# Summing the eight factors of a matrix on TensorE as stacks of 16 rows by 8 factors, with a new order of the first steps

## The chip, the cores and the metric

The kernel runs on one core of a Trainium2 chip. The metric is the time of one execution on the device in microseconds (us). Times of single stretches come from one profiled execution, whose profile is called the page, and from questions put to its trace. PE is TensorE, PEld its weight load, DVE VectorE, ACT ScalarE, POOL GpSimd, SP SyncE.

## The reference

All data are float32. Eight batches of 1024 rows of 1024 numbers (x), a memory of 64 rows for each batch with a mask, eight factor matrices of 1024 x 1024 and a bias.

```
scores = (layernorm(x) @ memory^T) / sqrt(1024), masked
x = x + softmax(scores) @ memory
x = x + (sum over r of layernorm(x) @ factors[r]) / sqrt(8) + bias
```

The eight factors are applied to the same rows, so their sum W can be made once (33.5 MB are read for a matrix of 4.2 MB) and each row is multiplied by W alone.

## The kernel before

The 8192 rows are worked on in 16 groups of 512 rows: four tiles of 128 rows, numbered t, or two halves q of 256 rows. Two groups make up a batch and share its memory. A group goes through these steps: its rows are loaded (load_rows, and from group 2 on a second time in another layout by load_blocks); their mean and variance are taken; the rows are transposed; scores and softmax against the memory; read_out multiplies the weights by the memory; residual adds that to x in place; norm_sums and norm_squares (ACT, half a group each, with the last steps on POOL) take the second layernorm's statistics; normalize (ACT) writes the normalized rows h. For PE, h must stand transposed. In group 0 PE does this (transpose_h_pe, copies by ACT). From group 1 on relayout (L575) moves h by 16 transfers of 64 KB on SP's queue into a tile hb, and transpose_rows (DVE) transposes blocks of 32x32 into hT.

The product with W is done by a scheme with seven half-size products in place of eight (numbers 1 to 7, with sums s1 to s4 of quarters of hT by combine_rows and sums t1 to t4 of quarters of W). W's quarters and their combinations stand in seven tiles, wq: b11, b21, b22, t1, t2, t3, t4, each of 128 x 4 x 512. Products 2 to 5 are split once more into seven parts of a quarter of the size (combine_parts, part, give_part; combine_factors makes their right sides, on DVE); in the first groups product 5 is done whole instead. product (L614) needs b11 for number 1, t1 for 5, t2 for 6 and t3 for 7; t2, t3, t4, b21 and b22 need all of the factors. give adds a product to x, add_bias (POOL) adds the bias, store writes the tile.

The order is written out by hand. START is a table of steps, run once; it holds groups 0 and 1, the factors and the beginning of group 2. LOOP is a table run for each group g, with steps of the group before (p), the next (n) and the next but one (m). Each engine and each queue takes its instructions in the order of these tables, and SP issues all transfers but the first memory, the mask and the bias, which ACT issues. Every transfer gets one of eight completion semaphores in turn.

Room is given out by Slots, first returned first taken. There are ten large buffers of 1 MB (bigs) for factors, h, hb, hT, and the transposed or block-wise x, and eight PSUM banks (banks). A step that takes a buffer waits for the step that returned it.

The factors before: load_factor s r (L700) reads a quarter s of the rows of factor r, 1 MB in one transfer with 8 KB for each partition. The eight terms of a quarter are added in two ways, as the table says: add_factor (L706) adds two loaded tiles, or one to the sum so far, on DVE; sum_factor (L724) multiplies by the identity on PE, four matmuls of 512 columns that accumulate in four PSUM banks, and add_sums (L739) adds these on DVE. START has 12 sum_factor and 20 add_factor steps, and one of the relayouts of group 1 comes after the last load_factor, the other later still.

```
load_factor 2 0; add_bias 0 0 3; add_factor 2 3; part 0 4 2; load_factor 2 5;
combine_parts 0 4 2; add_factor 2 1; sum_factor 2 0; product 0 1 5; combine_rows 0 0 4;
add_factor 2 4; give_part 0 4 2; combine_parts 0 4 3; load_memory 2; load_rows 2 0;
normalize 1 0 1; relayout 1 0; add_factor 2 5; centre_memory 2; normalize 1 1 0; add_sums 2 1;
product 0 0 6; load_blocks 2 1; add_sums 2 0; add_bias 0 1 3; give 0 0 6; transpose_memory 2;
```

Of the kernel before, what the change touches and what calls it, by code (L numbers as in the profile page):

```python
# [24 lines left out]
load_rows 1 0; constants; load_rows 0 0; load_rows 0 1; load_rows 0 2; load_memory 0;  # L25
row_stats 1 0; load_rows 1 1; transpose_x_pe 0 0; row_stats 0 0; centre_memory 0; load_rows 0 3;
transpose_x_pe 1 0; load_rows 1 2; masks; transpose_memory 0; load_factor 0 5; add_factor 0 5;
row_stats 0 1; load_factor 1 6; transpose_x_pe 0 1; load_rows 1 3; row_stats 1 1; scores 0;
scores_back 0; row_stats 0 2; load_factor 1 3; transpose_x_pe 1 1; row_stats 0 3;
load_factor 0 2; softmax 0; load_factor 1 1; scores 1; row_stats 1 2; row_stats 1 3;  # L30
add_factor 1 6; weights_back 0; scores_back 1; read_out 0 0 0; add_factor 0 2; read_out 0 1 0;
softmax 1; read_out 0 0 1; residual 0 0 0; residual 0 0 1; load_factor 1 2; load_factor 1 0;
load_factor 0 6; read_out 0 1 1; load_factor 1 5; weights_back 1; norm_sums 0 0; add_factor 1 3;
residual 0 1 1; load_factor 1 7; residual 0 1 0; add_factor 0 6; add_factor 1 7; sum_factor 1 0;
add_factor 1 2; load_factor 1 4; sum_factor 1 1; norm_squares 0 0; read_out 1 1 0;
load_factor 0 7; load_factor 0 3; read_out 1 0 1; load_factor 0 4; normalize 0 0 0;
normalize 0 0 1; norm_sums 0 1; sum_factor 1 4; residual 1 1 0; load_factor 3 7; add_factor 0 7;
transpose_h_pe 0 0 0; read_out 1 0 0; residual 1 0 0; norm_squares 0 1; load_factor 3 5;
read_out 1 1 1; residual 1 0 1; sum_factor 1 5; transpose_h_pe 0 0 1; load_factor 0 0;
residual 1 1 1; add_sums 1 1; load_factor 0 1; add_sums 1 0; add_factor 0 3; combine_rows 0 0 1;  # L40
sum_factor 3 5; add_factor 0 1; norm_sums 1 1; sum_factor 3 7; normalize 0 1 0; sum_factor 0 4;
normalize 0 1 1; add_factor 0 0; load_factor 3 3; load_factor 3 2; sum_factor 3 3; norm_sums 1 0;
combine_rows 0 0 2; add_sums 0 1; load_factor 3 4; norm_squares 1 0; load_factor 3 6;
add_factor 3 2; transpose_h_pe 0 1 0; add_sums 0 0; load_factor 3 0; load_factor 3 1;
add_factor 3 4; load_factor 2 3; load_factor 2 6; load_factor 2 1; add_factor 3 0;
add_factor 3 1; normalize 1 0 0; transpose_h_pe 0 1 1; load_bias; product 0 0 5; load_factor 2 2;
give 0 0 5; sum_factor 3 6; load_factor 2 7; add_bias 0 0 2; norm_squares 1 1; load_factor 2 4;
combine_rows 0 1 1; product 0 0 1; combine_rows 0 0 3; add_factor 2 6; product 0 1 1;
add_sums 3 1; combine_parts 0 4 1; add_sums 3 0; sum_factor 2 2; give 0 1 1; give 0 0 1;
sum_factor 2 7; load_factor 2 0; add_bias 0 0 3; add_factor 2 3; part 0 4 2; load_factor 2 5;  # L50
combine_parts 0 4 2; add_factor 2 1; sum_factor 2 0; product 0 1 5; combine_rows 0 0 4;
# [16 lines left out]
scores_back 2; give 0 1 7; combine_factors 5; give_part 0 2 6; part 0 3 6; part 0 2 2;  # L68
row_squares 2 1; softmax 2; give_part 0 3 6; combine_parts 0 3 4; part 0 3 5; give 0 1 5;
part 0 2 7; give_part 0 2 7; part 0 3 2; store 0 3; add_bias 0 0 1; give_part 0 3 5;  # L70
give_part 0 2 2; add_bias 0 1 0; add_bias 1 0 2; part 0 3 7;
"""

LOOP = """
# [749 lines left out]
```

## Time and profile before

| what | value |
|---|---|
| times of 3 runs | 941.76, 943.79, 947.74 us; median 943.79 |
| span of the profiled execution | 939.8 us |
| PE busy | 916.9 us, 98% of the span |
| DVE, ACT, POOL busy | 783.4, 458.9, 265.2 us |
| DMA in the first four fortieths of the span (94 us) | 313, 421, 420, 421 GB/s |
| factor transfers | 32 of 1024 KB, median 11.4 us from issue to landing |
| relayout transfers | 480 of 64 KB, median 2.0 us from issue to landing |

The median of the times is 4.0 us above the profiled span. Busy time of PE is modelled from the starts of pipelined matmuls. A float32 matmul shows as two records, one for each pass, so the 48 matmuls of the 12 sum_factor steps are 96 rows of the profile. The rows that matter are shown with the prediction.

### The profile page before, as it was taken

To read this page: it belongs to the slowest core of one execution; us is meant where nothing else is said; L and a number is where in the kernel's file an instruction comes from. 1 tells how busy PE (TensorE), PEld (TensorE's weight loads), DVE (VectorE), ACT (ScalarE), POOL (GpSimd) and SP (SyncE) were. 2 spreads that over 40 slices of the span, in tenths; PEclk is the share of its full clock that TensorE was granted. 3 is DMA by queue.
4 is the path that set the end of the run, shared out by engine and by line. 5 is a ranking of instruction groups with operands and counts; after the bars stand their busy time and mean duration, and the time that the engine had idled before them with its cause. 6 is when DMAs were issued, how large, how long until landed. Compare 5 with 4: busy or idle time off the path is not lost.

```text
span 939.8 us, 11731 instructions
## 1 busy us (share of the span) xinstructions
PE 916.9 (98%) x3637; PEld 578.2 (62%) x3637; DVE 783.4 (83%) x1619; ACT 458.9 (49%) x836; POOL 265.2 (28%) x355
## 2 busy tenths in 40 slices
PE   4899999999999999999999999999999999999998
PEld 4444456756657565666656575665756666665766
DVE  4799998969698896969698897969889797979876
ACT  4573233638464463737555373836545464745100
POOL 0202023515133231514233151513323151423221
PEclk9999999999999999999999999999999999999999
DMA  8999767476574847467484846558484856641412
GB/s 313 421 420 421 205 160 187 139 164 177 142 188 122 213 136 165 146 166 191 122 199 125 206 145 159 157 148 202 121 193 139 182 153 157 171 134 57 128 46 89
DMA packets 93565, 167.04 MB, mean 178 GB/s; under 512 B 12352, under 2 KB 71872, under 8 KB 89408
## 3 DMA queue, kind: packets, MB, share of 16 engines
q1 hardware_dynamic: 93024, 165.20, 61.9%
q10 hardware_dynamic: 480, 1.12, 0.4%
q8 instruction: 28, 0.46, 0.2%
q14 instruction: 33, 0.27, 0.1%
HBM read 101.25 MB, written 33.55 MB: 143 GB/s over the span
## 4 chain that ended last, share of the span: by engine, by line
PE 92%; DMA 6%; DVE 1%; ACT 1%; issue 0%; SPq 0%; POOL 0%; DVEq 0%
PE yu L621 34%; PE ro L496 6%; PE y5u L671 6%; PE y2u L671 6%; PE y4u L671 6%; PE y3u L671 6%; PE scT L428 6%; DMA f<-in_L_ffn_factors_dram 5%; PE y3v L671 3%; PE y5v L671 3%; PE y2v L671 3%; PE y4v L671 3%; PE sum L734 2%; PE y3z L671 1%; PE y2z L671 1%; PE y5z L671 1%
## 5 line engine op out<-in xcount | busy, mean ns | idle before, releaser
L570 POOL TENSOR_TENSOR x<-x,bias_bc 128x512 f32<-128x512 f32 x128 | 170.2, 1342 | 130.0 <-DVE x L685 51.6
L589 DVE STREAM_TRANSPOSE hT<-hb 128x1024 f32<-128x1024 f32 x60 | 72.7, 1231 | 59.7 <-DMA hb<-h 55.4
L532 ACT ACTIVATE junkz<-x 128x1024 bf16<-128x1024 f32 x64 | 67.6, 1057 | 109.0 <-DVE x L504 108.0
L621 PE MATMUL yu<-t,s 128*128 128x512 f32 x256 | 115.3, 593 | 1.9 <-DVE t L750 1.9
L621 PE MATMUL yu<-b,hT 128*128 128x512 f32 x256 | 114.9, 592 | 0.0
L621 PE MATMUL yu<-t,hT 128*128 128x512 f32 x256 | 112.6, 592 | 0.0
L563 ACT ACTIVATE h<-x,nb,rstd 128x512 f32<-128x512 f32 x128 | 96.5, 825 | 24.8 <-POOL rs L335 13.5
L504 DVE SCALAR_TENSOR_TENSOR x<-ro,rden,x 128x512 f32<-128x512 f32 x128 | 88.6, 746 | 13.2 <-PE ro L496 13.0
L634 DVE SCALAR_TENSOR_TENSOR x<-yu,x 128x512 f32<-128x512 f32 x128 | 82.8, 678 | 3.3 <-PE yu L621 3.2
L621 PEld LDWEIGHTS yu<-t,hT 128*128 128x128 f32 x256 | 48.6, 190 | 54.0 <-issue 52.6
L385 DVE STREAM_TRANSPOSE xT<-xb 128x256 f32<-128x256 f32 x224 | 81.6, 411 | 0.0
L621 PEld LDWEIGHTS yu<-t,s 128*128 128x128 f32 x256 | 48.5, 190 | 50.6 <-issue 46.3
L543 ACT ACTIVATE junky<-x,zm 128x1024 bf16<-128x1024 f32 x64 | 73.5, 1149 | 11.1 <-POOL zm L330 8.5
L621 PEld LDWEIGHTS yu<-b,hT 128*128 128x128 f32 x256 | 48.6, 190 | 48.4 <-issue 46.9
L330 POOL TENSOR_SCALAR zm<-zs 128x2 f32<-128x2 f32 x28 | 9.8, 351 | 223.9 <-ACT junkz L532 223.9
L347 ACT ACTIVATE junk<-x 128x1024 bf16<-128x1024 f32 x56 | 58.9, 1052 | 26.1 <-DMA x<-in_x_dram 25.2
L359 ACT ACTIVATE junk<-x,nmean 128x1024 bf16<-128x1024 f32 x56 | 64.3, 1148 | 7.1 <-POOL nmean L330 4.9
L496 PE MATMUL ro<-mem,eT 64*128 64x512 f32 x256 | 64.8, 615 | 0.6 <-DVE x L504 0.4
L428 PE MATMUL scT<-xT,memT 128*64 128x256 f32 x512 | 58.8, 382 | 0.0
L685 DVE SCALAR_TENSOR_TENSOR x<-y3u,x 128x256 f32<-128x256 f32 x64 | 26.7, 418 | 37.5 <-PE y3u L671 30.3
L428 PEld LDWEIGHTS scT<-xT,memT 128*64 128x64 f32 x512 | 35.3, 137 | 21.1 <-issue 4.3
L734 PE MATMUL sum<-f,ident 128*128 128x512 f32 x96 | 42.8, 597 | 2.3 <-DMA f<-in_L_ffn_factors_dram 2.1
(148 smaller groups left out, 1631.5 us busy)
## 6 DMA issues: line engine op xcount, KB each, us to landing
x<-in_x_dram SPq DMA_DIRECT2D x64, 512.0 KB, 3.5
f<-in_L_ffn_factors_dram SPq DMA_DIRECT2D x32, 1024.0 KB, 11.4
out_dram<-x SPq DMA_DIRECT2D x64, 512.0 KB, 3.1
hb<-h SPq DMA_DIRECT2D x480, 64.0 KB, 2.0
xb<-in_x_dram SPq DMA_DIRECT2D x112, 256.0 KB, 7.5
mem<-in_ctx_dram SPq DMA_DIRECT2D x14, 256.0 KB, 6.3
mem<-in_ctx_dram ACTq DMA_DIRECT2D x2, 256.0 KB, 9.4
bias_bc<-in_L_ffn_bias_dram ACTq DMA_DIRECT2D x1, 512.0 KB, 8.1
```

What stands on the lines that cost most here:

```text
L385: nc.vector.transpose(xT[:, 2 * e + c].rearrange("p (t j) -> p t j", j=Q), xb.rearrange("p t (k e i c) -> p e c t k i", e=NC // 2, i=2, c= ...
L428: nc.tensor.matmul(ps[ts(h, M), : 2 * P], mT[:, c, :], st["xT", g, h][:, c, :], start=(c == 0), stop=(c == NC - 1),)
L496: nc.tensor.matmul(ps, eT[ts(h, M), q, :], m[ts(h, M), ts(n, H)], start=True, stop=True)
L504: nc.vector.scalar_tensor_tensor(xt, st.pop(("ro", g, q, n, h)), rden[:, k : k + 1], xt, ALU.mult, ALU.add)
L532: nc.scalar.activation(junk, st["x", g, 2 * h + q], AF.Copy, accum_out=s1[:, h : h + 1])
L543: nc.scalar.activation(junk, st["x", g, 2 * h + q], AF.Square, bias=nmean[:, h : h + 1], accum_out=ss[:, h : h + 1])
L563: nc.scalar.activation(to, fr, AF.Identity, bias=nb[:, h : h + 1], scale=rstd[:, h : h + 1])
L570: eng.tensor_add(xt, xt, bias_bc[:, ts(k % 2, H)])
L589: nc.vector.transpose(st["hT", g, q][:, h].rearrange("p c (t j) -> p t c j", j=Q), hb[:, h].rearrange("p t (c i) -> p t c i", i=Q),)
L621: nc.tensor.matmul(ps, lhs[:, c, :], wq[right][:, c, :], start=(first and c == 0), stop=(c == KH - 1), skip_group_check=True,)
L634: nc.vector.scalar_tensor_tensor(xt, st["y", g, q, key], ISR, xt, ALU.mult, ALU.add)
L671: nc.tensor.matmul(ps, lhs[:, c, :], right[:, c, :], start=(first and c == 0), stop=(c == 1), skip_group_check=True,)
```

## The change

load_stack takes the place of load_factor. A stack is one transfer's worth of 16 rows of all eight factors: partition 8k + r holds row k (of the 16) of factor r, 4 KB. A load_stack fills one buffer of 1 MB with two stacks, by two transfers of 512 KB. add_stack takes two buffers (four stacks) and adds the eight factors within each stack by a matmul with a 0/1 matrix of 128 x 32 (stack0 for the even, stack1 for the odd of 32 output rows); the four stacks go to four strips of 32 partitions of the same PSUM bank, for both halves of the columns: 8 matmuls. Two add_stacks (i = 0, 1) complete two banks. take_sums moves these into wq: b11, b21 and b22 by copies on ACT, t1 and t2 by subtractions on DVE straight from PSUM. subtract_factors makes t3 and t4. add_factor, sum_factor and add_sums are gone.

START is written anew. Its first part, up to the first steps of the parts of group 0, is shown below. In it both relayouts of group 1 stand among the load_stacks: 19 of the 32 come ahead of relayout 1 0, four between the two, nine after relayout 1 1. Products 1 and 5 of group 1 are done whole and stand ahead of the last add_stack. The memory is loaded ahead of the mask. LOOP holds the same steps in another order (so product 6 of half 0, and part 3 4's combine_parts, have moved over the loop's end into the next round). s2 gets a buffer for each half, in the room of mask8f.

```diff
+load_rows 0 1; load_rows 0 2; load_rows 0 0; load_memory 0; constants; load_rows 0 3;
+row_stats 0 0; row_stats 0 1; load_rows 1 0; centre_memory 0; transpose_x_pe 0 0; load_rows 1 2;
+transpose_x_pe 0 1; masks; row_stats 1 0; transpose_memory 0; row_stats 0 2; load_stack 0 0 0 1;
+load_rows 1 1; load_rows 1 3; load_stack 0 1 0 1; row_stats 1 1; scores 0; load_stack 1 0 0 1;
+row_stats 0 3; transpose_x_pe 1 1; row_stats 1 2; scores_back 0; transpose_x_pe 1 0; softmax 0;
+scores 1; weights_back 0; scores_back 1; load_stack 0 0 0 0; read_out 0 0 0; row_stats 1 3;
+read_out 0 0 1; load_stack 0 1 0 0; load_stack 0 1 1 0; load_stack 0 1 1 1; softmax 1;
+load_stack 0 0 1 0; load_stack 1 1 0 0; load_stack 0 0 1 1; add_stack 0 0 0; read_out 0 1 0;
+residual 0 0 0; read_out 0 1 1; residual 0 0 1; add_stack 0 1 0; norm_sums 0 0; residual 0 1 1;
+residual 0 1 0; norm_squares 0 0; load_stack 2 0 0 0; norm_sums 0 1; weights_back 1;
+norm_squares 0 1; read_out 1 0 1; residual 1 0 1; read_out 1 0 0; add_stack 0 0 1;
+normalize 0 0 0; residual 1 0 0; load_stack 1 1 0 1; load_stack 1 0 0 0; normalize 0 0 1;
+normalize 0 1 0; add_stack 0 1 1; transpose_h_pe 0 0 0; transpose_h_pe 0 0 1; take_sums 0 0;
+read_out 1 1 1; norm_sums 1 0; combine_rows 0 0 1; norm_squares 1 0; residual 1 1 1;
+normalize 0 1 1; load_stack 1 0 1 0; transpose_h_pe 0 1 0; add_stack 1 0 0; load_stack 1 1 1 1;
+transpose_h_pe 0 1 1; load_stack 1 0 1 1; combine_rows 0 0 2; load_stack 1 1 1 0;
+add_stack 1 1 0; add_stack 1 0 1; read_out 1 1 0; normalize 1 0 0; normalize 1 0 1;
+take_sums 1 0; residual 1 1 0; load_stack 2 1 1 1; load_stack 2 1 0 1; relayout 1 0;
+add_stack 1 1 1; take_sums 1 1; norm_sums 1 1; load_stack 2 0 0 1; combine_rows 0 0 3;
+take_sums 0 1; combine_rows 0 1 1; combine_rows 0 1 3; norm_squares 1 1; load_stack 2 1 0 0;
+transpose_rows 1 0 0; normalize 1 1 0; product 0 1 1; product 0 0 1; product 0 0 5;
+transpose_rows 1 0 1; load_stack 2 0 1 1; add_stack 2 0 0; load_stack 3 0 0 1; product 0 1 5;
+add_stack 2 1 0; give 0 1 5; normalize 1 1 1; relayout 1 1; load_stack 2 1 1 0; product 1 0 1;
+transpose_rows 1 1 0; combine_parts 0 4 1; combine_rows 0 1 2; take_sums 2 0;
+transpose_rows 1 1 1; load_stack 2 0 1 0; product 1 1 1; combine_rows 1 0 1; add_stack 2 0 1;
+load_bias; load_stack 3 0 0 0; add_stack 2 1 1; combine_parts 0 4 2; combine_rows 1 1 1;
+load_stack 3 1 0 0; take_sums 2 1; give 0 0 5; combine_rows 0 0 4; load_stack 3 1 0 1;
+load_stack 3 0 1 1; load_stack 3 0 1 0; product 1 1 5; give 0 1 1; add_stack 3 0 0; give 0 0 1;
+give 1 1 1; add_stack 3 1 0; load_stack 3 1 1 0; add_bias 0 0 3; add_bias 1 1 1; product 1 0 5;
+combine_factors 5; take_sums 3 0; subtract_factors 0; load_stack 3 1 1 1; add_stack 3 0 1;
+give 1 0 5; add_stack 3 1 1; add_bias 0 1 3; give 1 1 5; take_sums 3 1; load_rows 2 1;
+combine_factors 3; product 0 1 6; product 0 0 6; subtract_factors 1; part 0 4 2; load_memory 2;
+add_bias 0 1 2; add_bias 0 1 1; combine_factors 4; give 0 0 6; part 0 4 1; combine_parts 0 4 3;
+give 0 1 6; part 0 4 5; give_part 0 4 1; product 0 0 7; centre_memory 2; load_blocks 2 1;
+combine_parts 0 4 4; combine_factors 2; give_part 0 4 2; part 0 4 6; give 1 0 1; give_part 0 4 6;
...
@@ -175,10 +175,16 @@
     neghalf = const.tile([P, 4], F32, name="neghalf")
     nc.gpsimd.memset(neghalf, -0.5)
 
+    stack = [const.tile([P, 2 * P // R], F32, name=f"stack{i}") for i in range(2)]
+    for i in range(2):
+        nc.vector.memset(stack[i], 0.0)
+        nc.vector.tensor_reduce(
+            stack[i].rearrange("p (k i) -> p i k", i=2)[:, i], ident.rearrange("p (k r) -> p k r", r=R), AX.X, ALU.add
+        )
+
 
 
     mask8 = const.tile([B, P // M, M], mask.dtype, name="mask8")
-    mask8f = const.tile([B, P], F32, name="mask8f")
     maskT = const.tile([P, B], F32, name="maskT")
     valid = const.tile([P, B], F32, name="valid")
     bias_bc = const.tile([P, D], F32, name="bias_bc")
...
@@ -601,7 +606,7 @@
             ops["s1"] = work.tile([P, KH, P], F32, tag=f"s1{q if 5 in SECOND else ''}", name=f"s1_{g}_{q}")
             nc.vector.tensor_add(ops["s1"], ops["a21"], ops["a22"])
         if k == 2:
-            ops["s2"] = work.tile([P, KH, P], F32, tag="s2", name=f"s2_{g}_{q}")
+            ops["s2"] = work.tile([P, KH, P], F32, tag=f"s2{q}", name=f"s2_{g}_{q}")
             nc.vector.tensor_sub(ops["s2"], ops["s1"], ops["a11"])
         if k == 3:
             nc.vector.tensor_sub(ops["a21"], ops["a11"], ops["a21"])
@@ -697,60 +702,47 @@
         xs.back(("x", g, t))
 
 
-    def load_factor(s: int, r: int):
-
-        f = st["f", s, r] = bigs.take(("f", s, r), [P, 2, D], f"f_{s}_{r}")
-        src = factors[r].rearrange("(k e i c) n -> e k i (c n)", e=NS, i=2, c=2)[s]
-        nc.sync.dma_start(f.rearrange("p c n -> p (c n)"), src)
-
-    def add_factor(s: int, r: int):
-
-        c = slice(2 * (s % 2), 2 * (s % 2) + 2)
-        f = st["f", s, r]
-        if ("before", s) not in st:
-            st["before", s] = r
-            return
-        r0 = st["before", s]
-        before = None
-        if r0 is not None:
-            before, st["before", s] = st["f", s, r0], None
-        for n, key in enumerate(QUADS[s // 2]):
-            w = wq[key][:, c, :]
-            nc.vector.tensor_add(w, before[:, :, ts(n, H)] if before is not None else w, f[:, :, ts(n, H)])
-        if before is not None:
-            bigs.back(("f", s, r0))
-        bigs.back(("f", s, r))
-
-    def sum_factor(s: int, r: int):
-
-        terms = [line for line in read_table(START) if line.startswith(f"sum_factor {s} ")]
-        first, last = (line.split()[2] == str(r) for line in (terms[0], terms[-1]))
-        if first:
-            st["sums", s] = {
-                (c, n): banks.take(("sum", s, c, n), [P, 512], f"sum_{s}_{c}_{n}") for c in range(2) for n in range(2)
-            }
-        for c in range(2):
-            for n in range(2):
+    def load_stack(e: int, i: int, c: int, h: int):
+
+        f = st["f", e, i, c, h] = bigs.take(("f", e, i, c, h), [P, 2, D], f"f_{e}_{i}_{c}_{h}")
+        src = factors.rearrange("r (j k e i c) n -> e i c j k r n", j=NA, e=NS, i=2, c=2)[e, i, c]
+        for j in range(2):
+            nc.sync.dma_start(f[:, j], src[2 * h + j])
+
+    def add_stack(e: int, i: int, c: int):
+
+        if i == 0:
+            st["sums", e, c] = [banks.take(("sum", e, c, n), [P, 512], f"sum_{e}_{c}_{n}") for n in range(2)]
+        for n in range(2):
+            for j in range(NA):
                 nc.tensor.matmul(
-                    st["sums", s][c, n], ident, st["f", s, r][:, c, ts(n, H)], start=first, stop=last
+                    st["sums", e, c][n][ts(j, Q)],
+                    stack[i],
+                    st["f", e, i, c, j // 2][:, j % 2, ts(n, H)],
+                    start=(i == 0),
+                    stop=(i == 1),
                 )
-        bigs.back(("f", s, r))
-
-    def add_sums(s: int, n: int):
-
-        c2 = slice(2 * (s % 2), 2 * (s % 2) + 2)
-        for c in range(2):
-            w = wq[QUADS[s // 2][n]][:, 2 * (s % 2) + c, :]
-            nc.vector.tensor_add(w, st["sums", s][c, n], w)
-            banks.back(("sum", s, c, n))
-        w = {key: tile[:, c2, :] for key, tile in wq.items()}
-        if s < 2 and n == 0:
-            nc.vector.tensor_sub(w["t1"], w["t2"], w["b11"])
-        if s >= 2 and n == 1:
-            nc.vector.tensor_sub(w["t2"], w["b22"], w["t1"])
-            nc.vector.tensor_sub(w["t3"], w["t2"], w["b11"])
-        if s >= 2 and n == 0:
-            nc.vector.tensor_sub(w["t4"], w["b21"], w["t2"])
+        for h in range(2):
+            bigs.back(("f", e, i, c, h))
+
+    def take_sums(e: int, c: int):
+        ps = st.pop(("sums", e, c))
+        k = 2 * (e % 2) + c
+        w = {key: tile[:, k, :] for key, tile in wq.items()}
+        if e < 2:
+            nc.scalar.copy(w["b11"], ps[0])
+            nc.vector.tensor_sub(w["t1"], ps[1], w["b11"])
+        else:
+            nc.vector.tensor_sub(w["t2"], ps[1], w["t1"])
+            nc.scalar.copy(w["b21"], ps[0])
+            nc.scalar.copy(w["b22"], ps[1])
+        for n in range(2):
+            banks.back(("sum", e, c, n))
+
+    def subtract_factors(k: int):
+        w = {key: tile[:, ts(k, 2), :] for key, tile in wq.items()}
+        nc.vector.tensor_sub(w["t3"], w["t2"], w["b11"])
+        nc.vector.tensor_sub(w["t4"], w["b21"], w["t2"])
 
     def combine_factors(p: int, eng=nc.vector):
...
```

## The prediction

> **What bounds the kernel now.** I read the page's busy line and slices first, to find the engine that is never idle; then a table of stretches, to see where it does idle; then the order in time around the end of that stretch; then the groups, for prices.
>
> ```profile
> span 939.8 us, 11731 instructions
> PE 916.9 (98%) x3637; PEld 578.2 (62%) x3637; DVE 783.4 (83%) x1619; ACT 458.9 (49%) x836; POOL 265.2 (28%) x355
> ...
> PE   4899999999999999999999999999999999999998
> ...
> DMA  8999767476574847467484846558484856641412
> ```
>
> PE is the bound and misses only 22.9 us of the span. DMA is full only in the first four slices (94 us), where the 33.5 MB of factors come in.
>
> ```profile
> core 0: us, PE busy (x) PEld busy (x) DVE busy (x) ACT busy (x) POOL busy (x), PEclk, DMA share, GB/s
> ...
> 90.00:100.00 10.00, 9.70 (x26) 4.63 (x25) 9.96 (x12) 0.00 (x0) 0.68 (x1) 1.00 0.99 377
> 100.00:110.00 10.00, 8.11 (x20) 3.37 (x19) 8.77 (x12) 3.95 (x6) 1.46 (x2) 1.00 0.72 155
> 110.00:120.00 10.00, 10.00 (x36) 5.62 (x35) 9.79 (x17) 1.63 (x3) 0.00 (x0) 1.00 0.81 169
> ...
> 106.40:112.60 6.20, 5.13 (x20) 2.79 (x21) 6.02 (x8) 2.04 (x4) 0.00 (x0) 1.00 0.36 89
> ```
>
> Up to 110 us PE waits now and then (18.2 us in all); after that it is at 10.00 of 10 until the tail. The last row is the stretch in which only a relayout (hb<-h) moves: 0.36 of the DMA engines, against 0.99 to 1.02 while factors move.
>
> ```profile
> start us, us, engine line op out<-in xcount [idle before <-releaser]
> ...
> 101.99 3.60 PE L621 MATMUL yv<-t,s 128*128 128x512 f32 x8
> 107.47 2.84 PE L621 MATMUL yu<-t,s 128*128 128x512 f32 x6 [1.89 <-DVE t L750]
> ...
> 94.45 0.53 SPq L704 DMA_DIRECT2D f<-in_L_ffn_factors_dram  x1
> ...
> 97.92 14.59 SPq L580 DMA_DIRECT2D hb<-h  x16
> ```
>
> The last factor, issued at 94.45, lands at 102.31; VectorE adds it; product 6, the first that needs all factors, starts at 107.47. From there PE runs almost without a break to 935.1, and 4.7 us of adding and storing follow. So time = (start of product 6) + (PE work left then) + tail: 107.5 + 827.6 + 4.7 = 939.8. A change to the loading counts only through those terms. The 3 runs have a median of 943.8, so 4.0 us lie outside the profiled span; I add them at the end.
>
> ```profile
> L734 PE MATMUL sum<-f,ident 128*128 128x512 f32 x96 | 42.8, 597 | 2.3 <-DMA f<-in_L_ffn_factors_dram 2.1 <-ACT hT L401 0.2
> L428 PE MATMUL scT<-xT,memT 128*64 128x256 f32 x512 | 58.8, 382 | 0.0
> L719 DVE TENSOR_TENSOR b<-b,f 128x1024 f32<-128x1024 f32 x17 | 20.3, 1219 | 2.6 <-DMA f<-in_L_ffn_factors_dram 2.5
> ```
>
> **The sums.** Removed: 48 matmuls of 512 columns (two passes each: x96, 42.8 us), 32 adds of 1.22 us (39.0), 16 of 0.68 (10.9). Added: 16 add_stacks of 8 matmuls of 128x32. Four of these side by side have no row here. Two do: scores' 128x64 pairs (L428): the two of a pair start 7 ns apart and the next pair 0.216 us later, which is what one full pass of 256 columns takes alone (L671). If four overlap alike, a set of four costs two passes of 0.43 us, 0.87 with the starts, and an add_stack of two sets 1.75 us (28 us in all, 15 less than now). The other bound, each alone: 8 x 0.86 = 6.9 us. I take 1.75, the nearest row. The change of tile shape costs 0.09 us each way (a 256-column matmul is followed after 0.309 us instead of 0.216 where the shape changes): under 3 us in all. All of this lies before the gate, under the loading; only the last add_stack is on the path. The Trainium skill (TensorE: Matmul & The Clock Gate, Part 3) states 2.38x for three column tiles; at that efficiency four would take about 1.08 us instead of 0.87 and add_stack about 2.2, an estimate that only the last add_stack would feel, 0.4 us.
>
> take_sums moves PSUM to SBUF: 12 ACT copies of 0.59 us (row: L401), on an ACT that is half idle there, and 8 subtractions of 0.69 on VectorE; the 8 differences of 1.22 us for t1 to t4 become 4. VectorE loses about 49 us in all. That is worth little by itself: from last landing to product 6 it is now 5.2 us (adds 2.4, sums 1.3, t2 1.2, handovers); after, 1.75 + 0.7 + 0.2 = **2.65 us**. The two stack matrices (memset and reduction of 128x128, under 1 us) are made while VectorE waits for rows until 6.5.
>
> **The work left after the gate.** The new order does product 1 of group 1 (two times 3.43 us) and product 5 of group 1 (as products, not as 7 parts of 0.86) before the gate, and part 4 2 (0.86) after it. 827.6 - 6.9 - 6.0 + 0.9 = **815.6 us**.
>
> **When the last stack lands.** This decides. 4 KB packets take 161 ns against 312 for today's 8 KB, so a stack (two transfers of 512 KB) takes 2.58 us where a factor took 2.48. The Trainium skill (DMA: Bandwidth & Descriptors, Rules for kernel authors) asks for at least 1 MiB a transfer, which speaks against the halving. Were the fixed 2.0 us that the same page states (section Anatomy of one DMA) exposed for 32 more transfers, it would be an estimated 64 us. Rows of x are such 512 KB transfers and land 1.28 us apart, so I charge 0.1 us a stack.
>
> The SP queue, in its order: rows and memory (about 17.6 us; the mask's slow 512 B packets now come after the memory), then 18 stacks to load_stack 2 1 0 1: 17.6 + 18 x 2.58 = 64.0. Buffers: there are ten, an add_stack returns two. Of these 18 only the last two come late: their buffers are freed by add_stack 1 1 0, which is on PE behind transpose_h_pe 0 1 1, and that behind ACT's chain (norm_sums, norm_squares and normalize of group 0 and of half of group 1, each 2.5, 2.5 and 3.0 us by the timeline). From rows to that add_stack: 17.6 + 4.4 (copies of group 1's transposes) + 3.7 (scores 1) + 1.6 (weights_back 0) + 4.4 (read_out and two residuals) = 31.7; ACT then has three statistics steps of group 0, eT, the fourth, 4.6 of normalize, 2.1 of copies, a take_sums, two steps of group 1 and the rest of normalize: 24.4, to 56.1; transposes and add_stack 2.8, to 58.9. With 2.2 us from issue to first data (an x row lands 3.5 us after issue and takes 1.3), that is 2.3 us late: **66.3**.
>
> Then relayout 1 0 stands in SP's queue, 16 transfers, ahead of 13 stacks; before, both relayouts came after the last factor. Every transfer has one of eight completion semaphores and waits for the eighth before it (seen at 102.33, 104.53 and 106.41, where an hb is issued 0.02 us after an earlier landing). So the eighth hb is issued when the last stack ahead has landed; eight more go out at 0.635 us each (L580 row: 14.6 us for 16, half of them waiting); then the next stack, with 2.2 us to its first data: 5.7 + 2.2 = **7.9 us** with little moving, as in the 0.36 row. Bounds: 4.9 us (1024 packets of 1 KB at 76 ns on 16 engines) if it is only a transfer, 10 us if all 16 issues are exposed. Four stacks (10.3), relayout 1 1 with the same 7.9, nine stacks (23.2), bias (1.25): 66.3 + 7.9 + 10.3 + 7.9 + 23.2 + 1.3 = 116.9. Two other queues gain a wait. transpose_rows 1 1 stands on VectorE, waiting for its hb, ahead of take_sums 2 0, whose PSUM banks add_stack 2 0 1 needs; that is 3 us after the landing, and the stack which that add_stack waits for lands 6 us after it. load_bias waits on ACT's queue ahead of the copies of take_sums 2 1, which nothing needs before combine_factors 3. Buffers now come back one add_stack at a time. Today 38.9 MB at 0.42 MB/us from 20 us (5.9 MB then) would end at 98.6 and ended at 102.3; I add 2.3 of those 3.7 us: **119.2**, range 112 to 127.
>
> After the gate VectorE does combine_factors 3, 4 and 2 (each 4 x 0.69 us) and t3, t4 in one burst, 13 us, between the gives. PE's products 6 (6.9 us) and 7 cover most; I count 2.5 us of short waits at the parts (0 to 8). What waits behind them is only later parts. The loop's new order changes no amount; PE is already full there, so it can only lose: 0 to 5, taken as 0. The second s2 buffer removes a wait that costs nothing.
>
> **Sum.** 119.2 + 2.65 + 815.6 + 2.5 + 4.7 = 944.7; plus 4.0: **948.7**. The 15 us saved on PE are spent idle in front of a gate that moves from 107.5 to about 122, which gives back the 12 us of products done early.
>
> **Rivals.** About 1% is what a measurement of this kernel can tell from no change (three runs spread by 0.6%).
> - *The stream does not break at the relayouts.* For it: the hb transfers need only 4.9 us of DMA time each. Against: the 0.36 row. 64.0 + 9.8 + 33.5 + 1.3 = 108.6; 108.6 + 2.65 + 815.6 + 4.7 + 4.0 = 935.6. Chance 0.15.
> - *The four tiles do not run abreast, and PE becomes the bound ahead of the gate.* From product 1 1 1 (about 95) to the gate stand 3 products (10.3 us) and 6 add_stacks, so it decides from (24 - 10.3) / 6 = 2.3 us per add_stack. In pairs only (3.5 us): 95 + 10.3 + 21 = 126.3, about 5 us later and 954; one after another (6.9): 95 + 10.3 + 41.4 = 146.7 and about 973. For it: no row shows four. Against: the pairs of L428 overlap fully. Chance 0.10.
> - *VectorE falls behind after the gate*, with group 2's transposes in the same burst and scores 2 waiting for them: 8 to 10 us, 956. Against: it is 49 us lighter before. Chance 0.15.
> - *Rows 4 MB apart read slower.* No row shows such a source. 10% on 32 stacks is 8 us: 957. Chance 0.08.
>
> Forecast 0.52. Faster by over 1% needs the last landing before 107, the better half of the first rival: 0.09. Slower by over 1% (over 953.2) takes nearly all of the last three and the upper end of the forecast: 0.31. Range: from most of the first rival, 937, to 960.
>
> **To look for.** Right: DMA share near 1 until about 65, two dips of 6 to 10 us at the relayouts (about 66 and 87), last stack landing at 112 to 127, product 6 some 3 us later, PE at 10.00 of 10 from there, PE busy near 903. Wrong: no dips; sum matmuls of one bank not starting within some 30 ns of each other; product 6 before 110; PE idle in the loop.

## The result and the profile after

The changed kernel takes 1002.72 us (median of 4 runs, 998.04 to 1005.12) against 942.77 for the kernel before (4 runs): a ratio of 1.063, 95% interval 1.059 to 1.068. The profiled execution is the one of 998.04, its span 996.1 us.

The busy lines and slices of the page after, a slice now 24.9 us:

```profile
span 996.1 us, 12006 instructions
PE 937.4 (94%) x3785; PEld 578.0 (58%) x3785; DVE 729.6 (73%) x1565; ACT 463.4 (47%) x848; POOL 248.4 (25%) x355
...
PE   5777766999999999999999999999999999999998
...
PEclk9979889999999999999999999999999999999999
DMA  9998899674847465565747484747565574742312
GB/s 277 255 269 225 205 224 234 149 191 141 197 148 167 138 166 159 167 151 161 188 135 198 127 191 151 176 140 164 155 171 148 155 189 135 193 131 77 105 69 85
```

PE is at 9 from the eighth slice (174 us) on; before, it was there from the third (47 us). The whole loss lies ahead of that. The DMA line looks as full as before, and for longer. Only the line below it shows the trouble: 205 to 277 GB/s where before it was 420. The share of busy DMA engines alone does not say how much they move.

The table of stretches of the changed kernel (PE, PEld, DVE, ACT and POOL busy with their instructions, granted clock, DMA share, GB/s):

```profile
70.00:80.00 10.00, 6.32 (x43) 1.94 (x42) 1.57 (x3) 9.28 (x16) 1.08 (x3) 1.00 1.03 266
...
90.00:100.00 10.00, 8.20 (x20) 3.53 (x19) 2.84 (x5) 7.51 (x14) 1.08 (x3) 1.00 0.69 159
...
120.00:130.00 10.00, 1.94 (x5) 0.57 (x3) 1.18 (x2) 0.00 (x0) 0.00 (x0) 0.86 0.60 140
...
160.00:170.00 10.00, 6.80 (x26) 1.39 (x25) 7.25 (x10) 0.58 (x1) 0.00 (x0) 1.00 1.04 240
...
180.00:190.00 10.00, 10.00 (x42) 6.62 (x41) 9.86 (x21) 0.58 (x1) 1.39 (x1) 1.00 0.12 36
```

While stacks move, the share is 1.03 at 240 to 266 GB/s, so 1.05 MB take some 4.1 us. The two stretches with 0.69 and 0.60 are the relayouts. After the gate PE is at 10.00 of 10 here; in all it stands idle for 1.5 us from product 6 to its last matmul, 0.82 of them just before 199.1.

The chain of waits of the changed kernel up to the gate (start, length, what ended last):

```profile
79.07 16.04 DMA f<-in_L_ffn_factors_dram
95.11 0.02 issue
95.13 0.58 SPq L585
...
101.97 6.44 DMA f<-in_L_ffn_factors_dram
...
157.15 14.93 DMA f<-in_L_ffn_factors_dram
...
172.12 1.90 PE sum L718 x10
174.03 6.21 PE yu L626 x14
```

It is stacks on their way, an SP queue that issues hb (nine times from 95.13, eight times from 121.40), and stacks again. A stack's transfer is 14.9 us on its way at the end, because those ahead of it are slow. The last one lands at 172.08 and product 6 starts at 173.96.

### The profile page after: what moved, and what is told of

It is laid out like the page before. It is cut to its first block, busy times and chain, and to the rows that moved or that the text cites. A ratio compares the mean times of both kernels' runs of the same rounds, so it can differ in the third digit from the quotient of the medians.

```text
span 996.1 us, 12006 instructions
## 1 busy us (share of the span) xinstructions
PE 937.4 (94%) x3785; PEld 578.0 (58%) x3785; DVE 729.6 (73%) x1565; ACT 463.4 (47%) x848; POOL 248.4 (25%) x355
## 4 chain that ended last, share of the span: by engine, by line
PE 80%; DMA 14%; SPq 3%; DVE 1%; issue 1%; ACT 0%; ACTq 0%; DVEq 0%
PE yu L626 30%; DMA f<-in_L_ffn_factors_dram 12%; PE ro L501 6%; PE y4u L676 5%; PE scT L433 5%; PE y3u L676 5%; PE y2u L676 5%; PE y5u L676 5%; SPq L585 3%; PE y4v L676 3%; PE y5v L676 3%; PE y3v L676 3%; PE y2v L676 3%; PE sum L718 2%; PE y3z L676 1%; PE y2z L676 1%
## 5 line engine op out<-in xcount | busy, mean ns | idle before, releaser
L575 POOL TENSOR_TENSOR x<-x,bias_bc 128x512 f32<-128x512 f32 x128 | 168.1, 1327 | 274.4 <-DVE x L639 209.5
L626 PE MATMUL yu<-b,hT 128*128 128x512 f32 x256 | 117.4, 602 | 10.0 <-DVE hT L594 8.2
L626 PE MATMUL yu<-t,hT 128*128 128x512 f32 x256 | 115.1, 592 | 0.0
L568 ACT ACTIVATE h<-x,nb,rstd 128x512 f32<-128x512 f32 x128 | 95.8, 820 | 16.2 <-PE sum L718 11.9
L718 PE MATMUL sum<-f,stack 128*32 128x512 f32 x256 | 57.1, 687 | 27.4 <-DMA f<-in_L_ffn_factors_dram 27.4
L335 POOL TENSOR_SCALAR zm<-zs 128x2 f32<-128x2 f32 x28 | 6.3, 225 | 240.2 <-ACT junkz L537 240.2
L718 PEld LDWEIGHTS sum<-f,stack 128*32 128x32 f32 x256 | 10.4, 118 | 70.1 <-DMA f<-in_L_ffn_factors_dram 44.9
```

The lines of the kernel that those rows point to most:

```text
L568: nc.scalar.activation(to, fr, AF.Identity, bias=nb[:, h : h + 1], scale=rstd[:, h : h + 1])
L575: eng.tensor_add(xt, xt, bias_bc[:, ts(k % 2, H)])
L626: nc.tensor.matmul(ps, lhs[:, c, :], wq[right][:, c, :], start=(first and c == 0), stop=(c == KH - 1), skip_group_check=True,)
L718: nc.tensor.matmul(st["sums", e, c][n][ts(j, Q)], stack[i], st["f", e, i, c, j // 2][:, j % 2, ts(n, H)], start=(i == 0), stop=(i == 1),)
```

## The experiments

All are the changed kernel with one thing altered, except where another is named. near, rk, near_pool and the kernels whose names begin with four were run four times, the others once. Where the text that goes with a run says that W is another matrix, only the times are meant. The first question was why a stack takes 4.1 us. The packets say it too: 4 KB took 161 ns in rows of x before, and 267 ns (median from 20 to 60 us) in the stacks.

| kernel | what a transfer reads | us | GB/s, 20 to 40 us | packet, ns (median, 20 to 60 us) | last landing |
|---|---|---|---|---|---|
| changed | 16 rows, 64 KB apart, of 8 factors | 1002.7 | 255 | 267 | 172.1 |
| near | 16 neighbouring rows of 8 | 1003.2 | 245 | 285 | 177.4 |
| slots | 16 rows, 96 (later 80, 72, 68) KB apart, of 8 | 1002.6 | 245 | 278 | 176.3 |
| rshift | places 4 MB less 4 (later 32, 128, 384) KB apart | 1002.5 | 251 | 280 | 174.1 |
| half | 8 neighbouring rows of both halves of 8 | 1008.0 | 251 | 289 | 180.2 |
| pad | as near and half, steps off the powers of two | 1003.7 | 245 | 280 | 178.1 |
| rk | the rows of the changed kernel, factor by factor | 1054 to 1113 | 172 | 159 | gate 243.8 |
| two | 64 rows, 64 KB apart, of 2 | 959.1 | 409 | 160 | 133.1 |
| far | 2 that are 16 MB, 4 that are 8 MB apart, 2 and 4 neighbours | 959.0 | 409 | 160 | 133.2 |
| many | 128 rows of 1, then 2, 4, 8 factors | 969.8 | 409 | 160 | 144.4 |
| four | 32 neighbouring rows of 4 | 955.8 | 409 | 162 | 131.0 |

**Rows of one place, modulo 64 KB?** All 128 rows of a transfer lie 64 KB or a multiple apart. near takes that away:

```
-factors.rearrange("r (j k e i c) n -> e i c j k r n", ...)
+factors.rearrange("r (e c j i k) n -> e i c j k r n", ...)
```

> Same work as the changed kernel, but a stack is 16 neighbouring rows of each factor (64 KB in one piece, eight pieces 4 MB apart) in place of 16 rows that lie 64 KB apart; columns of h and rows of W keep their natural order. Theory A (a packet is slow because all 128 rows of a transfer lie at the same place modulo 64 KB): 4 KB packets fall from 265-280 ns to about 160, a stack takes 2.6 us, the two dips at the relayouts stay, last landing near 119 us, about 948 us. Rival B (slow because the eight factors lie 4 MB apart) and rival C (slow because of half-size transfers of 4 KB packets): packets stay at 265-280 ns and the time near 1003 us.

It took 1003.2 us (ratio 1.064, 1.061 to 1.067), with packets even longer. (The memory of later batches also got the new column order, which its scores don't share, so those are others.) Theory A falls. slots moved the rows over 2, 4, 8 and 16 places instead:

```
+step = 16 + (8, 4, 2, 1)[n // 8]        # n counts the load_stacks
+src = rows[:, : 15 * step + 1 : step].rearrange("r k n -> k r n")
```

> Still eight factors 4 MB apart and rows far apart, but the step between the 16 rows is 96, 80, 72 and 68 KB for the first, second, third and last eight load_stacks in place of 64 KB, so that a transfer's rows lie at 2, 4, 8 and 16 places modulo 64 KB (other rows are read, so W is another matrix). Theory A: packets get shorter with the number of places; if one place gives 4.1 us a stack and two give twice as much, the engines' own 2.6 us is reached at once, else in steps between 270 and 160 ns; the time between 945 and 975 us. Rivals B and C: all packets stay at 265-280 ns, near 1003 us.

From 20 to 160 us the medians of 20 us each stay between 266 and 280 ns, and the time is 1002.6 us.

**Eight factors?** two leaves the 64 KB step and changes nothing but the number of factors in a transfer, two in place of eight:

```
+src = factors.rearrange("(s r) (k e i c) n -> e i c s k r n", r=2, ...)[e, i, c]
 nc.sync.dma_start(f[:, j], src[2 * h + j])
```

> The same bytes as the changed kernel, but each transfer takes 64 rows, 64 KB apart, of two factors in place of 16 rows of eight (the sums then add other rows, so W is another matrix). Theory A: all 128 rows of a transfer still lie at one place modulo 64 KB, packets stay at 265-280 ns and the time near 1003 us. Rival B: only two pieces 4 MB apart, so packets fall to 200 ns or less and the time by 20 us or more. Rival C: unchanged.

```profile
20.00:40.00 20.00, 18.11 (x138) 9.80 (x134) 12.04 (x26) 14.72 (x38) 3.38 (x7) 1.00 1.03 409
```

This stretch of two has the same share, 1.03, and 409 GB/s in place of 255. Rival C falls as well, since packets and transfers are as large and as many. many asks from how many factors on:

```
+few = (1, 2, 4, 8)[n // 8]              # factors in a transfer
```

> Each transfer takes its 128 rows from one factor in the first eight load_stacks, from two in the next eight, then from four, and from eight in the last eight (other rows are added, so W is another matrix). Theory B1 or B2 alike: 160 ns a packet with one and two, 270 with eight; four tells whether it grows in steps (B2: about 200) or sets in between four and eight. Stacks on the way: 8 x 2.6 + 8 x 2.6 + 8 x 2.6 to 4.1 + 8 x 4.1, so the gate 20 to 35 us earlier than in the changed kernel, about 965 to 985 us.

Two stretches of many, with one to two factors a transfer, and with eight:

```profile
20.00:40.00 20.00, 17.00 (x128) 9.05 (x124) 10.94 (x23) 15.83 (x40) 3.52 (x7) 1.00 1.03 409
120.00:130.00 10.00, 6.64 (x24) 1.05 (x16) 1.14 (x2) 0.59 (x1) 3.94 (x3) 0.80 1.03 244
```

With one, two and four the packets took 159 to 164 ns, with eight 271 to 275 (medians of 10 us): it sets in above four and at eight at the latest. Both sorts of transfer stand in one execution here, so no difference between kernels or between executions can have made it.

**Which property of eight factors?** rk reads the same rows in another order, so that neighbouring packets are 64 KB apart in place of 4 MB:

```
-"r (j k e i c) n -> e i c j k r n"
+"r (j k e i c) n -> e i c j r k n"       # and the 0/1 matrix to match
```

> The changed kernel with the same rows in each stack, but partition 16r + k in place of 8k + r (and the 0/1 matrix to match): a transfer takes the 16 rows of one factor, then those of the next, so that neighbouring packets are 64 KB apart in place of 4 MB. Theory B1 (it is the jump from packet to packet that costs): packets fall from 270 to about 160 ns and the time to that of the forecast, about 949 us. Theory B2 (it is that a transfer touches eight factors at all, in any order): packets stay at 270 ns and the time near 1003 us.

Neither happened. It takes 1054 to 1113 us in its four runs, with packets at 159 ns; the stretch from 40 to 60 us shows why:

```profile
40.00:60.00 20.00, 12.11 (x50) 3.21 (x50) 6.55 (x12) 12.47 (x25) 2.16 (x6) 0.83 0.51 207
```

The share is 0.51: half of the engines do all of the work, and a packet of 159 ns on eight engines gives those 207 GB/s. The transfer's outermost dimension is 8 now (r) where it was 16 (k). The Trainium skill (DMA: Bandwidth & Descriptors, Rules for kernel authors) states just that: an outermost dimension below 16 confines a transfer to at most as many engines. The row agrees. So rk could not tell the two theories apart, since half of the engines don't reach the rate in question. half has an outermost dimension of 16, with eight packets from one factor under each index. It is built on each engine taking one index; no trace here names the engine of a packet, so that split is not shown.

```
+src = factors.rearrange("r (b x k) n -> (r b) x k n", b=2, k=8)
+nc.sync.dma_start(f[:, j], src[:, 16 * e + 8 * i + 4 * c + 2 * h + j])
```

> The changed kernel, but a transfer takes 8 neighbouring rows out of each half of the eight factors (partition 16r + 8b + k, 16 pieces of 32 KB, 2 MB apart), so that all 16 engines work and each has its 8 packets from one factor (rows go to other places of W, so W is another matrix). Theory B1 (a packet is slow when an engine's own sequence goes round eight distant places): about 160 ns a packet at full share, last landing 131 to 135, about 957 us. Theory B2 (slow when eight factors are read at the same time by all 16 engines, whichever engine reads which): 270 ns, near 1000 us.

```profile
20.00:40.00 20.00, 16.57 (x120) 9.54 (x118) 9.72 (x22) 12.91 (x35) 2.43 (x4) 1.00 1.03 251
```

251 GB/s at a share of 1.03, 1008.0 us: B1 falls if the engines split the transfer so. Then it is what all engines read together, not what one engine reads in turn. far asks whether the distance does it:

```
+kind 0: "(a s) ... -> s k a ...", s=4     # r and r + 4
+kind 1: s=2                               # r, r + 2, r + 4, r + 6
+kind 2, 3: two and four neighbours
```

> Which factors a transfer reads, changed by quarters of the load_stacks: two that are 16 MB apart (r and r + 4), then four that are 8 MB apart (r, r + 2, r + 4, r + 6), then two neighbours, then four neighbours (rows 64 KB apart; other rows are added, so W is another matrix). Theory B5 (what counts is how many places a transfer reads at once: four are served at full rate, eight are not): 160 ns a packet in all four quarters, about 957 us. Theory B6 (what counts is the span, or factors that lie 16 MB apart disturbing each other, which four neighbours never have): 200 to 290 ns in the first two quarters, 160 in the last two, 975 to 985 us.

```profile
20.00:40.00 20.00, 17.71 (x134) 9.55 (x130) 11.63 (x25) 15.10 (x39) 3.52 (x7) 1.00 1.03 409
```

This is the quarter with two places 16 MB apart. The packets take 159 to 161 ns (medians) in all quarters; with four places 8 MB apart eight transfers in a row land within 11.0 us, which is 381 GB/s. So it is not the distance. That leaves the eight rows agreeing in their low addresses. rshift and pad take that away, first in the step between factors, then in both steps:

```
rshift: +step = D - (1, 8, 32, 96)[n // 8]           # rows from place to place
pad:    +step = (D - 1, D - 17, D // 2 - 1, D // 2 - 9)[n // 8], neighbouring rows
```

> Eight factors a transfer as in the changed kernel, but the step from factor to factor is 4 MB less 4 KB, 32 KB, 128 KB and 384 KB in the first, second, third and last eight load_stacks (other rows are added, so W is another matrix). Theory B3 (the cost is that the eight rows agree in their low address bits, being exactly 4 MB apart): packets fall to 160 to 200 ns, at the latest with the larger shifts, and the time to 950 to 970 us. Theory B4 (the cost is the distance alone): packets stay at 270 ns, near 1003 us.

> Both steps off the powers of two at once: in the first and second eight load_stacks 16 neighbouring rows of eight places that are 4 MB less 4 KB and less 68 KB apart; in the third and fourth 8 neighbouring rows of 16 places that are 2 MB less 4 KB and less 36 KB apart (other rows are added, so W is another matrix). Theory B7 (places a power of two apart meet in the same part of the memory, and the earlier kernels each left one such step in): 160 to 200 ns a packet, 957 to 970 us. Theory B5 (it is the number of distant places, eight or more): 270 to 290 ns in all four quarters, 1000 to 1008 us.

```profile
20.00:40.00 20.00, 17.02 (x109) 10.24 (x106) 9.68 (x21) 11.89 (x33) 2.43 (x4) 0.91 1.03 245
```

This is pad. Both stay where they were: 1002.5 and 1003.7 us, 251 and 245 GB/s. The Trainium skill (DMA: Bandwidth & Descriptors, Latency and other measured facts) tells of copies at a row pitch of 4 MiB that fell to 103 GB/s and came back to full rate with 4 KiB of padding. The fall agrees in kind (245 to 255 GB/s here against 409), the cure doesn't: four places 4 MB apart need none, and eight are not helped by it. Shown is that stretches in which only such transfers move run at 239 to 269 GB/s where a transfer draws on eight (or sixteen) places 2 to 4 MB apart, and at 381 to 409 where it draws on up to four, with every row step and offset that was tried. What in the memory path makes the difference stays open; five to seven places, and eight places within one factor, were not tried.

**The change with fast stacks.** four computes the same sums from 32 neighbouring rows of four factors. One 128x32 matrix serves both accumulations, and these are now the two halves of the factors:

```
+src = factors.rearrange("(i r) (e c j k) n -> e i c j k r n", ...)[e, i, c]
+nc.vector.tensor_reduce(stack4, ident.rearrange("p (k r) -> p k r", r=NA), AX.X, ALU.add)
+stack = [stack4, stack4]
```

> A mended form of the change that computes the whole reference: a transfer takes 32 neighbouring rows of four factors (partition 4k + r), one 128x32 matrix serves both, and the two accumulations of a strip are now the two halves of the factors in place of two sets of 16 rows; as many transfers, packets and matmuls. Theory B1 (the packets of one engine go round eight factors; four are few enough): 160 ns a packet, a stack 2.6 us, last landing near 133 us as in the two-factor kernel, about 959 us. Rival (the forecast's sum holds once a stack takes 2.6 us): last landing 119 us, about 949 us. Rival B2, if near rows or the order matter after all: near 1003 us.

955.8 us (ratio 1.014, 1.012 to 1.016), last landing 131.0. So the slow stacks cost 172.1 - 131.0 = 41 of the 53 us by which the last stack missed the forecast (39 by two, whose last stack lands at 133.1), and the change is slower by 1.4% even without them. The rest is in four's chain of waits:

```profile
63.52 8.85 DMA f<-in_L_ffn_factors_dram
72.37 0.02 issue
72.39 0.58 SPq L583
...
98.89 2.04 DMA hb<-h
...
102.51 6.77 PE yu L624 x8
109.28 3.64 PE sum L716 x32
112.92 0.07 SPq L708
112.99 0.04 issue
113.03 7.25 DMA f<-in_L_ffn_factors_dram
```

After the stack that lands at 72.37, SP issues hb until 78.5. At 98.89 the second relayout is awaited, by the transposes and so by product 1 1 1, which stands on PE ahead of add_stack 2 0 1; that one's buffers let the next stack go at 113.03. I took the product's place for the cause and moved it:

```
-product 1 1 1; combine_rows 1 0 1; add_stack 2 0 1; ... product 1 1 5;
+combine_rows 1 0 1; add_stack 2 0 1; ... product 1 1 1; product 1 1 5;
```

> The mended kernel with product 1 1 1 moved behind add_stack 2 0 1 and 2 1 1 on TensorE, and transpose_rows 1 1 behind take_sums 2 1 on VectorE; nothing else. Theory P (the rest of the miss is mostly this: add_stack 2 0 1 stands behind a product that waits for the second relayout, so buffers come back late): the wait of the stacks near 111 us goes, last landing 131 becomes 124 to 126, about 949 to 951 us. Rival Q (the two gaps in SP's queue alone set it): within 2 us of 955.8.

961.8 us (1.022, 1.020 to 1.023): slower by 6. Theory P falls. The timeline of PE of that kernel (start, length, line; in brackets the idle time before and its releaser):

```profile
91.24 3.70 PE L623 MATMUL yu<-b,hT 128*128 128x512 f32 x8
109.13 5.83 PE L715 MATMUL sum<-f,stack 128*32 128x512 f32 x32 [14.19 <-DMA f<-in_L_ffn_factors_dram]
117.04 3.67 PE L623 MATMUL yu<-b,hT 128*128 128x512 f32 x8 [2.08 <-DVE hT L591]
```

add_stack 2 0 1 starts at 109.1 as it did in four (109.2), because its own stack, issued behind the second relayout, lands only then. The product had only filled that wait; now PE is idle for 14.2 us and has the product still to do. The edit moved one thing more: with the transposes gone from their place, ScalarE gets to the bias at 92.36 in place of 104.07, SP's issues of the second relayout then wait 2.9 us for the bias to land, and end 2.3 us later than in four. A chain names one of several things that end together.

Three kernels took the relayouts out of SP's way, by another queue:

```
-nc.sync.dma_start(hb[ts(a, Q), :, t, :], ...)
+(nc.gpsimd if g == 1 else nc.sync).dma_start(...)      # four_act: nc.scalar
```

> The same, with the two relayouts of group 1 issued by GpSimd in place of SP. If the two gaps in the stream come from the 32 issues in SP's queue, they go and the last stack lands 10 to 16 us earlier: 943 to 949 us. If the next stack waits for the relayout in any case (it takes the buffer of h), half of that or less: 953 to 959 us.

> The same with ScalarE issuing these relayouts. SP's queue is free as with GpSimd, but ScalarE stands 10 us at each, ahead of norm_squares and normalize of group 1 and of the copies of the sums: if SP's queue alone is the cause, 943 to 949 us as with GpSimd; if ScalarE is late for the second relayout and the products of group 1, 950 to 960 us.

> The same order, the two relayouts issued by GpSimd, and the buffers of h given to hT in place of the next stacks. If the queue's gaps and the product's place are the two causes and add, the stream flows but for waits on buffers: last landing 113 to 119 us, 938 to 944 us. If the ten buffers are short while h, hb and hT of both groups are held (six of them), GpSimd's slower relayouts hold them longer: 947 to 953 us.

| kernel | us | ratio, 95% interval | last landing |
|---|---|---|---|
| four | 955.8 | 1.014 (1.012 to 1.016) | 131.0 |
| four_pool | 954.5 | 1.013 (1.011 to 1.015) | 128.4 |
| four_act | 966.6 | 1.025 (1.022 to 1.028) | 140.9 |
| four_order_pool | 957.1 | 1.017 (1.015 to 1.018) | 130.7 |

four_act is slower than either of the two ranges of its text, and so is four_order_pool; four_pool lies in the second of its two. near_pool had done the same on slow stacks:

> As the kernel with neighbouring rows, and the two relayouts of group 1 are issued by GpSimd instead of SP. If the dips come from the 16 issues that stand in SP's queue, each of the two gaps of about 8 us goes and the gate comes 10 to 16 us earlier: about 935 us. If the next stacks wait anyway, because they take the buffer of h that the relayout gives back, or because GpSimd issues the transfers more slowly, the gaps stay and the time is that of the kernel with neighbouring rows within 5 us.

999.6 us against 1003.2. With GpSimd the relayouts take longer (8.4 us from issue to landing at the median in near_pool, 2.0 with SP), hold h and hb longer, and the next stack but one waits for h's buffer; SP's gap has become a wait on buffers. With ScalarE, its queue is taken up for 15.7 and 13.3 us by the 16 issues of each, ahead of a copy of b11 that product 0 0 1 needs: PE is idle for 15.5 us before 82.4. In four_pool no stack is issued between 64.8 and 79.3.

four_late puts both relayouts behind the last stack and group 1's transposes and products behind the gate. (combine_factors 5 has changed a quarter of t1 by then, so product 5 of group 1 is another.)

```
-load_stack 2 1 0 1; relayout 1 0; ...  normalize 1 1 1; relayout 1 1; ...
+load_stack 3 1 1 1; relayout 1 0; add_stack 3 0 1; ... add_stack 3 1 1; relayout 1 1; ...
```

> The mended kernel with both relayouts behind the last stack in SP's queue, and the transposes and products 1 and 5 of group 1 behind the gate. Nothing stands in the stream: last landing 102 to 106 us as in the kernel before, gate 105 to 109, but 12.9 us more of products after it: 940 to 945 us, the time of the kernel before. If VectorE, with the transposes of group 1 and the factors' sums in one burst after the gate, makes PE wait: 946 to 952 us.

967.9 us (1.028, 1.024 to 1.031). Nothing stands in the stream any more, and yet the last stack lands at 119.05, not 102 to 106. Its chain of waits:

```profile
70.07 6.28 PE yu L627 x14
76.34 3.43 PE yv L627 x8
79.78 1.85 PE sum L719 x16
81.63 3.63 PE yv L627 x8
85.26 1.92 PE sum L719 x16
87.19 0.50 SPq L711
87.69 0.05 issue
87.74 7.13 DMA f<-in_L_ffn_factors_dram
```

Group 0's products stand ahead of the add_stacks on PE, and stacks wait for the buffers: none is issued between 68.8 and 81.7. In four this wait lay under the first relayout. After the gate, at 122.64, four_late needs 844.1 us in place of 822. Of these 22 us, four whole products of group 1 are 13.7 (the 12.9 expected had product 5 in seven parts). PE is idle for 4.9 us more than in the changed kernel, 4.4 of them before transposes that wait for hb, since SP has 32 issues to make up to 134.5. Two groups of matmuls take 2.4 us longer than the same groups elsewhere (7.82 and 5.37 us, against 7.13 and 3.67). four_late_first moves two add_stacks ahead of those products (and combine_factors 5 behind product 1 1 5):

```
+add_stack 2 0 0; add_stack 2 1 0; product 0 1 1; product 0 0 1; product 0 0 5; ... product 0 1 5;
```

> The kernel with the relayouts behind the last stack (four_late), with add_stack 2 0 0 and 2 1 0 moved ahead of product 0 1 1, and combine_factors 5 behind product 1 1 5. Theory R (with the relayouts gone, what holds the stream is that these two add_stacks, whose buffers the next stacks need, stand behind 17 us of group 0's products on TensorE): the wait of the stream between 67.6 and 81.7 us becomes 76 at the latest and the last landing moves from 119 to 110 to 114 us. Rival S (ten buffers are short whatever the order): last landing within 2 us of 119. The time stays above that of the mended kernel in both, since group 1's products come after the gate.

It took 970.9 us (1.033, 1.030 to 1.035). The wait ended at 76.5, against the 76 of Theory R, but the last stack landed at 117.4: the next stacks then waited from 81.4 to 95.0 for an add_stack behind product 0 1 5. Theory R holds for the one wait and fails in its sum. The landing within 2 us of 119 is what Rival S had named, ten buffers that are short whatever the order. The trace shows an add_stack behind a product at this wait too, so one more order does not settle which of the two it is. No version here beats the kernel before.

## Why the prediction was wrong

It had the right place (the time follows the gate), and one of its rivals had the cause, at a fifth of its size. Two steps of the sum failed: the price of a stack, and the waits on buffers.

- *Work after the gate.* 815.6 + 2.5 + 4.7 = 822.8 was forecast; from 173.96 to 996.1 it took 822.2, and 822.2 in two. Right: the time follows the gate. The 2.5 us of short waits in it were 1.5.
- *From last landing to product 6.* 2.65 forecast, 1.88 measured (173.96 - 172.08). Right within 0.8.
- *Four tiles abreast.* Right: an add_stack (16 passes) takes 1.85 us in the row at 79.78 of four_late, against 1.75 and the changes of shape, and the matmuls of one set start mostly 6 or 7 ns apart; the rival is out.
- *VectorE behind after the gate.* Out: PE was busy 16.00 of the 16 us from 174 to 190 and idle for 1.5 us in all after the gate, where the rival had 8 to 10.
- *A stack costs 0.1 us more than a factor.* This step failed. The row it rested on was x, in which a transfer reads one piece of 512 KB; no row read from eight places. A stack took 4.1 us, not 2.58: 41 us at the last landing. Half the size of the transfers was not the reason: in four, with 512 KB transfers too, they land 1.28 us apart, as x does. Nor did the 2.0 us that the prediction quotes for each transfer show, from a section on transfers that GpSimd issues; these are SP's. The rival "rows 4 MB apart read slower" was priced at 10% with nothing behind that number, while the packets show 66% (267 against 161 ns). Its chance of 0.08 and price of 8 us left nearly all of this outside the range.
- *Relayouts at 7.9 us each.* About right one by one: in four the stack after the first landed 11.8 and the stack after the second 10.9 us after the one before, where 2.56 is usual, so 9.3 and 8.4 lost. The rival that the stream does not break there is out: the DMA share in the changed kernel falls to 0.69 and 0.60. What they cost together is not their sum: without them (four_late) the stream ended 11.9 us earlier, not 17.7.
- *Waits on buffers at 2.3 + 2.3 us.* Too small. My sum without relayouts and with fast stacks is 119.2 - 15.8 = 103.4; four_late measured 119.05, so 15.7 us are missing. The trace shows the waits behind products of group 0, above all from 68.8 to 81.7, where none is issued; that they are all of the 15.7 is not shown. (The sum has 18 + 4 + 9 = 31 of the 32 stacks. If the first, which stands among the rows, is not in the 17.6 us for these, 2.6 of the 15.7 are that stack.) I had followed PE's queue as far as transpose_h_pe and add_stack 1 1 0, but not past product 0 1 1 to add_stack 2 0 0.
- *PE busy near 903.* 937.4: the sums were at 57.1 us instead of 28, since many start in twos and tens as data come, and some in stretches of a lower clock (0.63 from 40 to 60 us). It costs nothing before the gate, as PE waits for stacks there.
- *4.0 us outside the span.* Too much by some 2 us. The runs on record lie 1.7 to 2.8 us above their own spans (998.04 against 996.1); the rest of the 4.0 was the spread between runs.

The sum again, from what was measured: 119.2 + 41.1 (slow stacks) + 15.7 (buffers) - 3.9 (relayouts that lay over those waits: 15.8 forecast, 11.9 measured) = 172.1. Its terms are differences between the runs, so it closes by itself. It shows how large each part is and is no test of the causes: the first is shown by many and two, those behind the other two terms are read from chains of waits.

## What to carry to other kernels

Price a transfer from a row that reads from as many distant places at once, not only in pieces of the same size; where there is none, that is the open term of the sum and its bounds must be wide. Read GB/s beside the DMA share, which was 1.03 at 245 and at 409 GB/s. When buffers are few, follow each engine's queue up to the step that gives them back, and expect a removed wait to uncover the one beneath.

## What the runs showed of the hardware

- Transfers that read from eight or sixteen places 2 to 4 MB apart ran at 239 to 269 GB/s with a DMA share near 1.03; those that read from one, two or four places at 381 to 409 (two places 16 MB apart 409, four places 8 MB apart 381). Single packets of 4 KB took 267 to 289 ns and 159 to 162 ns (medians from 20 to 60 us).
- A transfer whose outermost dimension is 8 ran at a share of 0.51 and 207 GB/s.
- PE's granted clock was 0.50 from 50 to 60 us in the changed kernel, where PE ran ten matmuls, and 1.00 from 174 to 190, where it was never idle. Product 1 1 1 took 6.77 us in four after 7.3 us of idling, with a clock of 0.56 from 100 to 110, against 3.43 to 3.70 elsewhere.
